# Layer 3's last two chunks of nodes summed over fetched lists of neighbours instead of a dense product

## The chip, the cores and the metric

The kernel runs on one core of one Trainium2 chip. The metric is device time in microseconds (us), lower is better. Times are the median of several executions; the profile is of one more execution.

## The reference, cut to what matters

A graph of 2708 nodes has 512 features per node (`x`) and a symmetric adjacency matrix `adj` of zeros and ones, with each edge drawn at a rate of about 0.006. Four layers run one after the other, each followed by a residual sum and a layer norm.

```python
x = _layernorm(x + L0(x, adj, deg))   # relu(((a_norm @ x) + x) @ W + b)
x = _layernorm(x + L1(x, adj))        # (dis * adj * dis) @ x @ W.T + b
x = _layernorm(x + L2(x, adj))        # two attention passes, below
x = _layernorm(x + L3(x, adj))

# L2, one pass: scores over all pairs, softmax, times adj, sum
a = softmax(Wh @ Ws.T) * adj; x = leaky_relu(a @ Wh + x)
# L3, eight heads whose weights lie side by side: in effect
L3 = (adj @ x) @ W + b
```

Layer 3 so needs, for every node, the sum of `x` over its neighbours, then one product with a 512x512 matrix.

## The kernel before, in words

The nodes are padded to 22 blocks of 128 (the last block has 20 nodes). They are taken in six chunks `CH` of 512, 512, 512, 512, 384 and 276 nodes: chunk 3 is blocks 12 to 15, chunk 4 blocks 16 to 18, chunk 5 blocks 19 to 21.

**Dense layers (0, 1 and 3).** `Fast.step` (line 1114) goes over steps (layer, chunk k, group g). A group is three or four blocks of neighbours. The adjacency lies in DRAM as bytes (`masks`, written in layer 0). `load` (762) fetches the bytes of a group two steps ahead on SP, `prepare` (807) casts them on ACT one step ahead to a page `m` (float32r, 128 neighbours x the chunk's nodes), and `multiply` (893) sums `x` over them on TensorE (PE): `x` is split into `hi` and `lo` so that the fast float32r product keeps its precision, and each block takes four matmuls for each of them, one for each 128 features. After six groups `evict` (967) copies the four sums to `ht`, already turned (features on the partitions). `project` (984) multiplies them with `W` one step later, and `combine`, `finish` (1056) and the DMA of the result follow. `residual` (1013) loads the rows for the residual sum (`xres`) on POOL's queue.

**Lists.** In layer 1 `index` (1183) builds for every block i the lists `givers[:, i, t]` of the neighbours that its nodes have. A block's twelve lists hold 128 row numbers each. Four of them (`t` from 8) serve the whole block, eight serve a quarter of 32 nodes (two lists each). `lists_of` (480) orders them: four single lists, then two groups with one list of each quarter. The last block has three single lists.

**Layer 2.** For each attention pass, `scores`, `soften` and `weigh` run as a pipeline over the chunks: PE computes the scores of chunk k, DVE and ACT make the softmax of chunk k-1 (times the byte mask `a`), and chunk k-2 is summed over its lists. `soften` (1606) writes the weights `s` with SP to a table `pairs` in DRAM, beside copies of the features; `fetch` (1660) gathers from it, with one indirect DMA per list on POOL, rows that hold both a neighbour's weights and its features. `weigh` (1715) multiplies the two parts of such a row on PE. A group of four quarter lists is four matmuls with 32 columns of weights side by side. At a chunk's end, `end` and `normalize` (1779) make the result rows `r` and write them to DRAM (`saved[2]`, the tile `x` of the DMA `x<-r`), from which layer 3 loads its rows again (`x<-x`).

**Order.** `Ordered` (54) keeps every engine's instructions in the order in which Python issues them, so each queue (PE, DVE, ACT, POOL and SP) works in order. All instructions are recorded at line 71. Where PE's order is a mixture of two strands, Python keeps a clock of estimated times (`advance`, `later`) and issues a piece when that clock says that its inputs are there. Layer 3's first three chunks are begun inside layer 2's end (`early`, 604), since their first 16 neighbour blocks are ready then. Their groups 4 and 5 and all of chunks 3 to 5 come after it.

**Buffers.** `page` gives one of 82 buffers of 2 KB per partition. A new tile takes a buffer whose earlier tile has no more users in the program, and its first writer waits for those users. `wide` gives one of 11 buffers for gathered rows, `bank` one of eight PSUM banks in two halves of four.

The lines at layer 2's end that write the result:

```python
for (i, _, _), (r, _) in zip(ch.blocks, ch.ends):
    self.nc.sync.dma_start(self.k.saved[2][i], r)
    self.made[i] = r
```

Of the kernel before, what the change touches and what calls it, by code (L numbers as in the profile page):

```python
# [8 lines left out]
FP = mybir.dt.float32  # L9
# [32 lines left out]
FAR = 4096  # L42
PAGES, WIDES = 82, 11
TWO = 3
LN_EPS = 1e-5
DEG_EPS = 1e-8
SLOPE = 0.01
# [40 lines left out]
class Kernel:  # L88


    def __init__(self, ctx, tc, x_in, x_t, adj, adj_t, w0, b0, w1, b1, w2, w2_t, w3, b3, out):
        self.tc, self.nc = tc, tc.nc
        nc = self.nc
        self.ctx = ctx
        self.x_in, self.x_t, self.adj, self.adj_t, self.out = x_in, x_t, adj, adj_t, out
        self.w0, self.b0, self.w1, self.b1, self.w2 = w0, b0, w1, b1, w2
        self.w2_t, self.w3, self.b3 = w2_t, w3, b3
        const = ctx.enter_context(tc.tile_pool(name="const", bufs=1))
        self.small = ctx.enter_context(tc.tile_pool(name="small", bufs=4))
        scratch = ctx.enter_context(tc.tile_pool(name="scratch", bufs=1, space=DRAM))  # L100
        tile_ = lambda name, shape, dt: const.tile(shape, dt, tag=name, name=name)
        self.ident = tile_("ident", [P, P], FP)
        self.ones = tile_("ones", [P, P], FP)
        self.ones_b = tile_("ones_b", [P, P], BF)

        self.rdeg = tile_("rdeg", [P, NB], FP)
        self.dis = tile_("dis", [P, NB], FP)
        self.nbad = len(CH) * NB
        self.bad = tile_("bad", [P, self.nbad + NB], FP)


        self.feeds = tile_("feeds", [P, NB, QUARTERS, NB], BF)
        self.givers = tile_("givers", [P, NB, LISTS], I32)

        self.base = tile_("base", [P, QUARTERS], FP)
        self.upto = tile_("upto", [P, P], BF)
        self.node = tile_("node", [P, 1], FP)
        self.block = tile_("block", [P, NB], BF)
        self.since = tile_("since", [P, P], BF)
        self.saved = [  # L120
            [scratch.tile([P, D], FP, tag=f"x{s}_{i}", name=f"x{s}_{i}") for i in range(NB)]
            for s in range(3)
        ]
        self.between = [
            scratch.tile([P, D], FP, tag=f"y_{i}", name=f"y_{i}") for i in range(NB)
        ]

        self.masks = [
            scratch.tile([P, NB, w], U8, tag=f"mask{k}", name=f"mask{k}")
            for k, (_, w) in enumerate(CH)  # L130
        ]

        self.turned = [
            [
                scratch.tile([P, DC, w], FP, tag=f"t{s}_{k}", name=f"t{s}_{k}")
                for k, (_, w) in enumerate(CH)
            ]
            for s in range(2)
        ]
# [345 lines left out]
    return rest + [[q * ONLY + t for q in range(QUARTERS)] for t in range(ONLY)]  # L485


def cost(columns):

    return 4 * columns / 2400  # L490
# [25 lines left out]
class Fast:  # L516
# [17 lines left out]
    def run(self):  # L534
        kernel, nc = self.k, self.nc
        with ExitStack() as ctx:
            pool = lambda name, bufs, **kw: ctx.enter_context(
                self.tc.tile_pool(name=name, bufs=bufs, reuse_waits="tile", **kw)
            )
            self.pages, self.wides = pool("pages", PAGES), pool("wides", WIDES)  # L540
            self.small, self.lists = pool("small_f", 4), pool("lists", 1)
            self.banks = [pool(f"banks{h}", 4, space=PSUM) for h in range(2)]
            given = [kernel.x_in[bass.ts(i, P), :] for i in range(NB)]
            l0 = Layer(0, given, kernel.w0, kernel.b0)
            l1 = Layer(1, kernel.saved[0], kernel.w1, kernel.b1)
            l3 = Layer(3, kernel.saved[2], kernel.w3, kernel.b3)
            self.attention = attention = Attention(self)
            self.jobs, self.due, self.other, self.beats = [], None, 1, 0
            run = Run(l0, l1)
            for t in range(len(run.seq)):  # L550
                self.step(run, t)
            attention.project(attention.layers[0], 0)
            for g in range(3):
                self.ends(run, g)
                if g == 1:
                    attention.project(attention.layers[0], 1)


            run = Run(l3)
            run.seq = [(l3, k, g) for k in range(TWO) for g in range(4)]  # L560
            run.seq += [(l3, k, g) for g in (4, 5) for k in range(2)]
            run.seq += [(l3, k, g) for k in range(2, TWO) for g in (4, 5)]
            run.seq += [(l3, k, g) for k in range(TWO, len(CH)) for g in range(len(GROUPS))]
            attention.run(self.early(run))
            for j in range(*GROUPS[5]):
                l3.rows[j] = attention.made[j]
            for t in range(4 * TWO, len(run.seq)):
                self.step(run, t)

            ly, k = run.before  # L570
            parts = self.project(ly, k)
            for some in (parts[:-1], parts[-1:]):
                made = []
                for i, n, ps in some:
                    made.append((i, n, self.combine(ly, k, len(made), i, n, ps)))
                self.finish(ly, k, made)
# [230 lines left out]
    def prepare(self, ly, k, g, between=None, late=False):  # L807
# [7 lines left out]
        for j, at in zip(range(*GROUPS[g]), ats):  # L815
            if k == 0:
                self.halve(ly, j)
            m = self.page(f"m{ly.number}_{k}_{j}", FR)
            nc.scalar.copy(m[:, :cw], at[:, :cw])
            ms.append(m)  # L820
            if between:
                between()
                between = None
# [7 lines left out]
        if ly.number == 1:  # L831
            at = ly.done.pop(("bytes", k, g))
            if late:
                return lambda: self.note(k, g, at)
            self.note(k, g, at)

    def note(self, k, g, at):

# [54 lines left out]
    def multiply(self, ly, k, g, only=None, ds=range(DC)):  # L893
# [9 lines left out]
        if blocks[-1] == NB - 1:  # L903


            blocks = blocks[:-1]
            for x in (ly.hi, ly.lo):
                for d in range(DC):
                    few = slice(d * QW, (d + 1) * QW)
                    nc.tensor.matmul(  # L910
# [102 lines left out]
    def residual(self, ly, k):  # L1013
        for i, _, _ in blocks_of(k):
            t = self.page(f"xres{ly.number}_{i}")
            self.nc.gpsimd.dma_start(t, ly.source[i])
            ly.done["xres", i] = t

    def biased(self, ly, k):
# [94 lines left out]
    def step(self, run, t):  # L1114
# [5 lines left out]
            self.attention.blank()  # L1120
        if ly.number == 1 and k == len(CH) - 1 and g in (2, 3, 4):
            self.attention.begin(g - 2)
        self.multiply(ly, k, g)
        if g == len(GROUPS) - 1 and k in ly.begun:
            self.evict(ly, k)
        wide = CH[k][1] == BANK
# [1 line left out]
            self.work("PE")  # L1128
        if run.before:
            self.ends(run, run.phase)  # L1130
            run.phase += 1
            if run.phase in ((3, 4, 5) if wide else (4,)):
                self.work("DVE")
# [234 lines left out]
class Attention:  # L1368
# [29 lines left out]
    def blank(self):  # L1398
# [3 lines left out]
        for pairs in (p for ly in self.pairs for p in ly):  # L1402
            self.nc.sync.dma_start(
                pairs[N:, : 2 * PAIR + D].rearrange("j (r d) -> j r d", d=D),
                t[:n, :].unsqueeze(1).to_broadcast([n, (2 * PAIR + D) // D, D]),
            )

    def begin(self, step):

# [369 lines left out]
    def normalize(self, ch):  # L1779
# [4 lines left out]
        def rest():  # L1784
            for _ in work:
                pass
            for (i, _, _), (r, _) in zip(ch.blocks, ch.ends):
                self.nc.sync.dma_start(self.k.saved[2][i], r)
                self.made[i] = r

        self.later(4, rest)
# [111 lines left out]
            yield from self.project_steps(ly, k)  # L1903


@with_exitstack
def kernel(
    ctx: ExitStack,
# [60 lines left out]
```

## Time and profile before

| | |
|---|---|
| median of 3 runs | 2306.28 us (2305.75 to 2307.77) |
| the profiled execution | 2307.16 us, span 2305.3 us |
| granted TensorE clock, mean | 0.995 |
| busy: PE, DVE, ACT, POOL | 2272.8, 1409.5, 675.9, 706.5 us |
| moved by DMA | 486.34 MB, mean 211 GB/s |
| gathers `g<-pairs,givers` on POOL | 510, mean 1031 ns; 6.1 us from issue to landing |

A line of the profile gives line, engine, operation, the tiles written and read (`out<-in`), shapes, a count, and the time. In a timeline the first two columns are start and length in us, and in brackets stands the engine's idle time before the piece with what ended it. In the chain of work that ended last the columns are start and length. "SPq" is the queue of SP, which issues DMAs; the length there is that of the issue, not of the transfer. A float32 matmul stands as two records.

Layer 1 ends near 605 us, layer 2's second pass runs from about 1250 to 2095, and after that only layer 3 is at work.

### The profile page before, as it was taken

The page shows a single profiled execution, that of the slowest core. Times are in us where ns is not written, and L with a number is a line of the kernel's source. Part 1 is how long each engine was busy: PE and PEld are TensorE (multiplying, and loading weights), DVE is VectorE, ACT ScalarE, POOL GpSimd, SP SyncE. Part 2 cuts the span into 40 slices and gives each one's busy share as a digit, 9 for nine tenths or more (in the row PEclk, how much of TensorE's full clock was granted, in tenths as well). Part 3 has the DMA queues.
Part 4 walks back from the last instruction along what each step waited for, and adds up shares of the span by engine and source line. Part 5 has one row for each costly group of instructions (what it writes and reads, how often), then busy time and mean ns, then how long its engine had stood idle before and what let it go on. Part 6 is the DMA issues. An engine that isn't in the chain of part 4 may idle for free.

```text
span 2305.3 us, 25891 instructions
## 1 busy us (share of the span) xinstructions
PE 2272.8 (99%) x8525; PEld 1292.4 (56%) x8525; DVE 1409.5 (61%) x2803; ACT 675.9 (29%) x1354; POOL 706.5 (31%) x822
## 2 busy tenths in 40 slices
PE   9999999999999999999999999999999999899997
PEld 6676777778644444443555444444443455476685
DVE  6777886786554538748667511228769789625523
ACT  7444352323111123222332200113222334342211
POOL 3333431111000001635466550001635467542000
PEclk9999999999999999999999999999999999999999
DMA  9966762222556505868699998504868799973311
GB/s 347 288 189 179 188 182 76 76 82 77 194 191 263 182 5 181 296 205 300 236 331 336 337 411 320 185 5 165 301 228 288 250 324 332 338 219 120 117 51 43
DMA packets 260929, 486.34 MB, mean 211 GB/s; under 512 B 40238, under 2 KB 126950, under 8 KB 260784
## 3 DMA queue, kind: packets, MB, share of 16 engines
q1 hardware_dynamic: 192128, 269.63, 33.6%
q0 software_dynamic: 68656, 214.96, 28.0%
q8 instruction: 69, 1.13, 0.2%
q14 instruction: 76, 0.62, 0.1%
HBM read 307.55 MB, written 176.92 MB: 210 GB/s over the span
## 4 chain that ended last, share of the span: by engine, by line
PE 87%; DMA 5%; DVE 4%; issue 2%; ACT 1%; POOL 1%; SPq 0%; DVEq 0%; POOLq 0%; ACTq 0%
PE sp L71 33%; PE acc L71 30%; PE mm L71 8%; PE z L71 6%; PE wst L71 6%; DMA at<-in_adj_t 1%; DMA g<-pairs,givers 1%; PE mix L71 1%; DMA xr<-y 1%; PE list L71 1%; DMA mask<-some 1%; DMA x<-x 0%; PE tr_x2t L71 0%; PE tr_x2b L71 0%; DVE xl L71 0%
## 5 line engine op out<-in xcount | busy, mean ns | idle before, releaser
L71 PE MATMUL sp<-xs,wst_sb 128*128 128x512 f32 (+3 forms) x2112 | 798.3, 545 | 0.0
L71 POOL DMA_INDIRECT g<-pairs,givers x510 | 525.6, 1031 | 870.6 <-DMA xr<-x 242.3
L71 PEld LDWEIGHTS sp<-xs,wst_sb 128*128 128x128 f32 (+1 forms) x2112 | 380.5, 186 | 407.7 <-issue 325.6
L71 PE MATMUL acc<-m,xh 128*128 128x512 f32 (+4 forms) x1584 | 567.8, 380 | 7.4 <-ACT m L71 5.8
L71 PE MATMUL acc<-m,xl 128*128 128x512 f32 (+4 forms) x1584 | 551.0, 366 | 3.5 <-DVE xl L71 3.5
L71 PEld LDWEIGHTS acc<-m,xh 128*128 128x128 f32 (+1 forms) x1584 | 288.6, 188 | 72.0 <-issue 21.6
L71 PEld LDWEIGHTS acc<-m,xl 128*128 128x128 f32 (+1 forms) x1584 | 289.1, 189 | 48.0 <-issue 5.5
L71 PE MATMUL acc<-g 128*32 128x512 f32 (+1 forms) x1020 | 265.7, 609 | 2.9 <-DMA g<-pairs,givers 2.5
L71 ACT COPY s<-sp 128x512 f32<-128x512 f32 (+2 forms) x252 | 132.6, 528 | 396.3 <-PE sp L71 389.8
L71 ACT ACTIVATE s<-s 128x512 f32<-128x512 f32 (+3 forms) x264 | 151.7, 580 | 323.5 <-DVE s L71 323.2
L71 DVE TENSOR_TENSOR top<-top,s 128x512 f32<-128x512 f32 (+2 forms) x240 | 149.4, 623 | 155.6 <-ACT s L71 153.9
L71 PE MATMUL mm<-w,ht 128*128 128x512 f32 (+1 forms) x528 | 224.1, 594 | 3.4 <-DVE ht L71 3.4
L71 ACT CAST m<-at 128x512 fp32r<-128x512 uint8 (+5 forms) x396 | 199.6, 567 | 60.9 <-DMA at<-mask 20.2
L71 DVE TENSOR_TENSOR s<-s,shift 128x512 f32<-128x512 f32 (+3 forms) x264 | 162.9, 620 | 38.2 <-ACT shift L71 38.2
L71 DVE TENSOR_TENSOR s<-s,a 128x512 f32<-128x512 f32 (+3 forms) x264 | 165.9, 628 | 15.1 <-DMA a<-mask 6.0
L71 DVE TENSOR_TENSOR sum<-sum,s 128x512 f32<-128x512 f32 (+4 forms) x252 | 156.9, 623 | 13.9 <-ACT s L71 13.9
L71 PEld LDWEIGHTS mm<-w,ht 128*128 128x128 f32 (+1 forms) x528 | 95.9, 186 | 121.2 <-issue 111.4
L71 PEld LDWEIGHTS acc<-g 128*32 128x32 f32 (+1 forms) x1020 | 75.8, 135 | 146.1 <-issue 118.0
L71 PE MATMUL z<-w,xt 128*128 128x512 f32 (+1 forms) x352 | 151.0, 596 | 0.0
L71 PE MATMUL wst<-xt,mixed 128*128 128x512 f32 (+2 forms) x384 | 150.5, 545 | 0.0
L71 POOL DMA_DIRECT2D x<-o x44 | 26.0, 597 | 354.8 <-DVE o L71 350.6
L71 PEld LDWEIGHTS wst<-xt,mixed 128*128 128x128 f32 x384 | 72.1, 190 | 71.0 <-issue 59.0
(168 smaller groups left out, 1495.3 us busy)
## 6 DMA issues: line engine op xcount, KB each, us to landing
pairs<-z_sb SPq DMA_DIRECT2D x84, 768.0 KB
pairs<-s SPq DMA_DIRECT2D x168, 256.0 KB
at<-in_adj_t SPq DMA_DIRECT2D x84, 256.0 KB
xres<-x POOLq DMA_DIRECT2D x44, 256.0 KB, 4.9
x<-o POOLq DMA_DIRECT2D x43, 256.0 KB, 2.9
pairs<-s SPq DMA_DIRECT2D x84, 128.0 KB
x<-x SPq DMA_DIRECT2D x37, 256.0 KB
at<-mask SPq DMA_DIRECT2D x32, 256.0 KB
```

The lines of the kernel that those rows point to most:

```text
L71: ins = call(*args, **kw)
```

## The change

Chunks 0 to 3 of layer 3 stay dense. For chunks 4 and 5 (six blocks, from `LISTED` = 16) the neighbours' rows are fetched by list, as in layer 2, with zeros and ones in the place of the attention weights.

A new table `sided` in DRAM has a row for every node: three times 128 values for an even block, 512 features, 128 values for the odd block after it. The values are the adjacency as float32.

- `blank` (layer 0) writes zeros to the pad rows, with four DMAs.
- `prepare` calls `give` for every cast page `m` of layer 1's chunks 4 and 5: two DMAs per page on SP, 88 in all.
- `normalize` in layer 2's second pass writes each block's `r` three times over into `sided`, with one DMA of 768 KB per block on SP, right behind the write to `saved[2]`.
- `Listed`, made when the attention has ended, fetches the 63 lists of the six blocks (10 ahead), beginning with block 21. While chunk 3's groups 1 to 5 run, `multiply` is called for one feature block d at a time, and `beside` puts lists in between, up to 1.6 times the dense piece's time. A block's sum leaves PSUM by DVE, is turned by four PE transposes, copied by ACT, and projected. `end_all` issues what is left, and chunk 3's projection comes after it.
- The residual rows of layer 3 are loaded on SP instead of POOL.

```diff
+DENSE = 4
+LISTED = CH[DENSE][0] // P
+SIDED = D + 2 * P
...
-            run.seq += [(l3, k, g) for k in range(TWO, len(CH)) for g in range(len(GROUPS))]
+            run.seq += [(l3, k, g) for k in range(TWO, DENSE) for g in range(len(GROUPS))]
             attention.run(self.early(run))
             for j in range(*GROUPS[5]):
                 l3.rows[j] = attention.made[j]
+            self.listed = Listed(self, l3)
             for t in range(4 * TWO, len(run.seq)):
                 self.step(run, t)
+            self.listed.end_all()
 
             ly, k = run.before
             parts = self.project(ly, k)
...
+            if ly.number == 1 and k >= DENSE:
+                self.give(k, j, m)
...
+    def give(self, k, j, m):
+
+        n, lo, cw = rows_of(j), 0, CH[k][1]
+        while lo < cw:
+
+            i = (CH[k][0] + lo) // P - LISTED
+            w = min(P if i % 2 == 0 else 2 * P, cw - lo)
+            at = i // 2 * SIDED + i % 2 * (D + P)
+            self.nc.sync.dma_start(
+                self.k.sided[j * P : j * P + n, at : at + w], m.bitcast(FP)[:n, lo : lo + w]
+            )
+            lo += w
...
-            self.nc.gpsimd.dma_start(t, ly.source[i])
+            (self.nc.sync if ly.number == 3 else self.nc.gpsimd).dma_start(t, ly.source[i])
...
-        self.multiply(ly, k, g)
+        if self.listed and k == DENSE - 1 and g > 0:
+            for d in range(DC):
+                self.multiply(ly, k, g, ds=[d])
+                self.listed.beside(few_us(k, g) / DC)
+        else:
+            self.multiply(ly, k, g)
+            if self.listed:
+                self.listed.advance(few_us(k, g))
...
                 self.nc.sync.dma_start(self.k.saved[2][i], r)
+                rows = self.k.sided[i * P : (i + 1) * P, P:]
+                self.nc.sync.dma_start(
+                    bass.AP(
+                        rows.tensor,
+                        rows.offset,
+                        [rows.ap[0], (SIDED, (NB - LISTED) // 2), (1, D)],
+                    ),
+                    r.unsqueeze(1).to_broadcast([P, (NB - LISTED) // 2, D]),
+                )
                 self.made[i] = r
...
+    def beside(self, us):
+
+        self.advance(us)
+        end = self.clock + 1.6 * us
+        while self.clock < end and self.weigh():
+            pass
...
+            nc.gpsimd.indirect_dma_start(
+                out=g[:, :width],
+                out_offset=None,
+                in_=self.k.sided[:, :],
+                in_offset=bass.IndirectOffsetOnAxis(ap=self.k.givers[:, i, t : t + 1], axis=0),
+                element_offset=(i - LISTED) // 2 * SIDED + first,
+            )
+            self.free = max(self.free, self.clock) + 1.3
+            self.fetched.append((g, self.free + 6))
...
+        for h, g in enumerate(gs):
+            lo, rows = (h * QW, QW) if side else (0, n)
+            e, z = (D + lo, 0) if odd else (0, P - lo)
+            nc.tensor.matmul(
+                self.acc[lo : lo + rows],
+                g[:, e : e + rows],
+                g[:, z : z + D],
+                start=first,
+                stop=last,
+            )
+        self.advance(1.1 if side else cost(D))
+        if last:
+            acc = self.acc
+            self.later(0, lambda: self.turn(i, n, acc))
+        self.fetch_ahead()
+        return True
...
+    def turn(self, i, n, acc):
+
+        nc, f = self.nc, self.f
+        r = f.page(f"sum3_{i}")
+        nc.vector.tensor_copy(r[:n], acc[:n])
+
+        def turn():
+            ps = f.bank(self.half, f"tr3_{i}", (P, DC, P))
+            for c in range(DC):
+                nc.tensor.transpose(
+                    ps[:, c, :n], r[:n, bass.ts(c, P)], self.k.ident[:n, :n]
+                )
+            t = f.page(f"turned3_{i}", FP, (P, DC, P))
+            nc.scalar.copy(t[:, :, :n], ps[:, :, :n])
+            x = self.ly.done["xres", i]
+            nc.vector.tensor_add(x[:n], x[:n], self.ly.bt[:n])
+            self.advance(0.45)
+            self.later(2, lambda: self.project(i, n, t))
+
+        self.later(2, turn)
```

## The prediction

> **What bounds the kernel now.** I read the page first. Its first line of busy times says that TensorE (PE) works nearly the whole span, so a change pays if it takes PE work away and costs only where it makes PE wait.
>
> ```profile
> PE 2272.8 (99%) x8525; PEld 1292.4 (56%) x8525; DVE 1409.5 (61%) x2803; ACT 675.9 (29%) x1354; POOL 706.5 (31%) x822
> ```
>
> Next came the chain of work that ended last, in order of time. Its last pieces are layer 3's end, with PE back to back:
>
> ```profile
> 2163.00 13.73 PE mm L71 x32
> 2176.73 37.30 PE acc L71 x176
> 2214.03 13.73 PE mm L71 x32
> 2227.76 28.38 PE acc L71 x176
> 2256.14 10.30 PE mm L71 x24
> 2266.44 18.06 PE acc L71 x143
> ```
>
> A float32 matmul stands as two records; four of them make the `mm` of a 128-row block (13.73 us for four blocks). The first `acc` piece is chunk 3's groups 1 to 5 (144 matmuls) and chunk 4's group 0 (32). The next is the rest of chunk 4 with chunk 5's group 0, the last is the rest of chunk 5. Chunk 5's `mm` follows and ends at 2292.97; DVE work and the write of the result fill the time to 2305.3.
>
> Where does PE wait before that? The windows of 5 us between 1780 and 2110 show holes almost only from 1950 to 2020, where layer 2 ends and layer 3 begins. Columns: PE, PEld, DVE, ACT, POOL busy, granted clock, DMA share, GB/s.
>
> ```profile
> 1975.00:1980.00 5.00, 3.25 (x7) 0.46 (x6) 0.00 (x0) 0.63 (x1) 3.78 (x5) 0.84 1.03 409
> 1995.00:2000.00 5.00, 5.00 (x23) 4.13 (x22) 4.83 (x14) 1.86 (x5) 0.00 (x0) 1.00 1.01 354
> 2000.00:2005.00 5.00, 1.58 (x7) 1.01 (x6) 4.59 (x11) 2.72 (x7) 0.00 (x0) 1.00 0.63 186
> ```
>
> The DMA engines are full (share about 1) from 1910 to 2000. The timelines of SP, ACT, DVE and PE in that stretch give the mechanism:
>
> ```profile
> 1987.17 2.63 SPq L71 DMA_DIRECT2D x<-r  x4
> 1991.66 3.02 SPq L71 DMA_DIRECT2D x<-x  x4
> ...
> 1992.32 0.62 ACT L71 CAST m<-at 128x512 fp32r<-128x512 uint8 x1 [6.96 <-DMA x<-r]
> ...
> 1993.32 0.55 DVE L71 COPY sum<-s 128x276 f32<-128x276 f32 x1 [0.54 <-DMA x<-r]
> ...
> 2003.54 0.61 ACT L71 ACTIVATE xh<-x 128x512 fp32r<-128x512 f32 x1
> ...
> 2004.71 0.50 PE L71 MATMUL acc<-m,xh 128*128 128x512 f32 x1 [3.42 <-ACT m L71]
> ```
>
> Chunk 3 of layer 2 writes its four result blocks `r` (12 to 15) at 1987. The new tiles `xl`, `m` and `sum` take over the pages of those `r` and wait until the writes have read them. After `sum`, DVE and ACT alternate over chunk 5's softmax, and only behind that does ACT prepare layer 3's next group, for which PE waits 3.42 us. So **the release of those pages sets when PE goes on**: 2004.71 is 11.4 us after `sum` could start.
>
> **What the Trainium skill says.** "DMA: Bandwidth & Descriptors", section Queues, rings and completion order: each of the 16 DMA engines goes round the queues that have work, and takes descriptors of one queue in ring order; a large write therefore holds back what SP issues behind it. The trace agrees: one 256 KB `xr<-y` that SP issued at 1973.53 landed 13.20 us later by the chain. "Perfetto Trace Analysis", section DMA Instruction — HWDGE (DVE, Sync): the profiled slice of such a DMA is the making of descriptors, not the movement of data. Here a `x<-r` slice is about 0.34 us and the page is free some 6 us later. "TensorE: Matmul & The Clock Gate", Part 1: an idle TensorE falls to half its clock until it has been busy again; here the clock was 0.66 in 2005 to 2010, after the 3.42 us.
>
> **Part 1: layer 3's end.** Removed: the dense sums of chunks 4 and 5. Chunk 4 is 5.5 (group 0) + 24.3 (28.38 less chunk 5's group 0 of 4.1), chunk 5 is 4.1 + 18.06: **51.9 us of PE**. Their 44 casts on ACT and mask loads on SP lay beside it: nothing.
>
> Added: blocks 16 to 20 have four single lists and two groups of four quarter lists each, block 21 three single lists. A single list is one float32 128x512 matmul, 0.858 us (13.73 / 16); a group of four took 0.99 to 1.12 in layer 2 (the `acc` x8 pieces of the chain between 1830 and 1949). So 23 x 0.858 + 10 x 1.1 = 30.7. Six turns of four transposes at 0.45 (`tr_top` x4 took 0.44): 2.7. The projections move but stay 18.0 in sum. **51.9 - 30.7 - 2.7 = 18.5 us less PE.**
>
> Do the lists arrive? 63 gathers on POOL, ten of them fetched ahead. The step of POOL is 0.95 + 0.30 = 1.26 us where no buffer is missing:
>
> ```profile
> 2036.14 0.95 POOL L71 DMA_INDIRECT g<-pairs,givers  x1 [0.30 <-PE acc L71]
> 2037.40 0.95 POOL L71 DMA_INDIRECT g<-pairs,givers  x1 [0.30 <-issue]
> ```
>
> The other 53 start when chunk 3's group 1 does and need 66.8 us, landing 6.1 us after issue (median of the page), so 73 us. PE has beside them 32 us of dense work, 30.7 of lists, 2.7 of turns and 18 of projections, 84 in all, and the order was built for 1.3 us per gather. I take 0.3 us of waiting. Exposed is the last block alone: PE waits for DVE's copy (0.95) and ACT's copy (0.8), with chunk 3's projection queued behind. The old wait of about 0.2 for `ht` goes. Three blocks instead of two are normalised ahead of the last one: 0.4. DVE and ACT queues delay some turns: 0.9, from nothing to 3. Sum: -18.5 + 0.3 + 1.75 - 0.2 + 0.4 + 0.9 = **-15.3, between -17 and -11**, the lower gain if a gather takes 1.4 us, as in 1840 to 1850.
>
> **Part 2: layer 2's copies.** Behind every `x<-r` SP issues a copy of 768 KB, 22 in all, 16.9 MB. At the 0.40 MB/us that the windows show for full DMA that is 42 us of DMA time, in bursts of 3.1 MB (7.7 us) at 1700, 1799, 1896, 1987, 2056 and 2102. SP's issue (0.36 us, as for `pairs<-z_sb`) is hidden, since SP mostly waits.
> - 1700 and 2056: idle DMA follows (0.13 in 1720 to 1725, 0.36 in 2060 to 2065) before anything is due: 0.
> - 1799: the masks `a` queue behind. They are due at 1819.66 and come near 1823; DVE is full until 1880, then has nearly 4 us to spare (1.19 busy in 1880 to 1885). 0.5, from 0 to 3.
> - 1896: about 2.4 MB fit into the gaps to 1925; 0.7 MB stays queued until 1987.
> - 1987: `r` of block 14 is free after 3.07 MB in SP's ring instead of 0.77, beside some 2.5 MB of gathers and the 0.7 left. 1987.3 + 14 (5.6 MB at 0.4) + 1.7 + 2 for the receipt (0.77 MB at half the rate is 3.9 of the 6 us seen) gives 2005, against 1993.3. PE goes on 11.4 us after that, at 2016. **+11.3, between +4 and +18**: +4 if SP's ring is served at full rate.
> - 2102: ACT's casts wait for those pages too; the page frees 2 to 6 us later, where the casts at 2108.75 are about 4 us ahead of PE's use at 2113.7: 0.5, up to 4.
>
> Sum **+12.3**.
>
> **Part 3: layer 1's writes.** 88 small DMAs on SP, each waiting for a cast on ACT. SP spends 88 x 0.45 = 40 us in some 85, so it keeps up, but what is queued behind is late. Near the end the casts of group 3 run at 589.43, their eight writes end near 593.5, then come eight weight loads (3.8 us), the last mask load at 597, six writes, and `xt` at 600.5.
>
> ```profile
> 589.43 1.38 ACT L71 CAST m<-at 128x276 fp32r<-128x276 uint8 x4
> ...
> 595.21 2.05 ACT L71 CAST m<-at 128x276 fp32r<-128x276 uint8 x6
> ```
>
> The mask lands near 601 (its cast is due at 594.66 + 4.1 + 3.0, the start of group 3 and the length of groups 3 and 4: 601.8) and `xt` near 605.5 to 606.5 (PE wants it at 604.90, "PE wst"). **+2, from 0 to 6.** Four blanking writes in layer 0, whose SP is busy with `at` loads: +0.3, up to 1.5. `xres` moves from POOL to SP: its waits for pages now hold up mask loads behind it, but chunk 3 runs at half its pace there, so they come in time: 0, up to 2.
>
> **Sum against the profiled execution** (2307.16 us, span 2305.3): -15.3 + 12.3 + 2.0 + 0.3 = -0.7, so 2306.5. That execution lies 0.9 above the median of the three runs (2306.28), so the sum on the median is 2305.6. I say 2306.
>
> **Rivals.**
> - *A wash (0.40)*: the sum above, with a range of its own of 2301.7 to 2310.9. Within 0.2% (4.6 us) is about what a measurement of this kernel can tell from no change.
> - *Faster: the copies are absorbed (0.27).* If SP's ring gets most of the DMA engines at 1987, `sum` starts 4 us later and the rest is as above: -15.3 + 5 + 2.3 = -8, **2298**. For it: three `x<-r` landed within 6 us of the first issue though DMA was full. Against: windows show 1.03 with 409 GB/s, nothing left to take.
> - *Slower: the copies crawl (0.33).* SP's ring moved only about 0.17 MB/us while gathers ran (0.41 less a gather of about 0.3 MB per 1.26 us). If gathers keep that share throughout, 3.8 MB take 22 us, `sum` starts at 2011, PE at 2022.5: +18 instead of +11.3, in all +6, **2312**. It decides once block 14's page frees more than 16 us late. For it: the 13.20 us for one small load. Against: POOL's gathers stop at 1993.7, so the engines are free for SP from about 2000.
>
> The smaller unknowns (layer 1, the turns, a slower gather) push up more than down. **Range 2296 to 2317**, from a little past the faster rival to a little past the slower one. Chances: faster 0.27, same 0.40, slower 0.33.
>
> **What would show it.** Right: chunk 3's lists and dense work fill PE without a hole over 1 us; the last `mm` ends about 16 us earlier relative to PE's start on chunk 3's group 0; a hole of 12 to 15 us in PE near 2001 to 2016, with `sum` waiting for the new copy. Wrong in the first part: waits for `g` in layer 3. Wrong in the second: `sum` starts within 5 us of 1993. Wrong in the third: PE waits before 610, over 5 us.

## The result and the profile after

The changed kernel takes **2323.73 us** (median of 4, 2322.02 to 2325.5). The kernel before takes 2307.03 (median of 4, among them the three that stand in the table of before). The ratio is 1.0073, with a 95% interval of 1.006 to 1.0086: slower by some 17 us. The profiled execution took 2322.38 us with a span of 2320.3, so it is 15.0 us longer in the span than the one of before. Helper lines have moved: what was L71 is L76, and L75 in kernels that only add a table to the kernel before.

The page's first line of busy times answers to the one shown of before:

```profile
PE 2263.3 (98%) x8323; PEld 1255.0 (54%) x8323; DVE 1412.1 (61%) x2812; ACT 661.4 (29%) x1313; POOL 756.0 (33%) x863
```

PE is busy for 9.5 us less, though the span is 15 us longer, so about 24.5 us of new idle time has come in. Busy time is not work alone: matmuls that a lowered clock stretches count in full, and the mean granted clock is 0.990 instead of 0.995. To find where the time went, I compare the start of the same PE instruction in both traces (chain of waits and timelines). The lag is by how much it starts later in the changed kernel:

| stage that ends there | before | after | lag | step of lag | predicted |
|---|---|---|---|---|---|
| layer 0's last products | 359.55 | 361.02 | 1.5 | +1.5 | +0.3 |
| layer 1 (first `wst`) | 604.90 | 616.58 | 11.7 | +10.2 | +2.0 |
| layer 2's end | 2016.20 | 2035.33 | 19.1 | +7.4 | +12.3 |
| chunk 3 of layer 3 begins | 2176.73 | 2195.87 | 19.1 | 0 | 0 |
| end of the span | 2305.3 | 2320.3 | 15.0 | -4.1 | -15.3 |

The last row belongs to the chain's end. In the changed kernel it reads, in order of time from the last list sums (start, length, what):

```profile
2260.70 9.12 PE acc L76 x43
2269.82 0.44 PE tr L76 x4
2270.26 2.65 PE acc L76 x8
2272.91 3.45 PE mm L76 x8
2276.38 0.70 DVE xres L76
2277.10 0.71 DVE st L76
2278.01 2.38 DVE xres L76 x4
2280.39 1.20 DVE ht L76 x2
2281.59 0.61 DVE sum L76
2282.24 1.13 PE tr L76 x4
2283.40 0.59 ACT turned L76
2284.03 16.33 PE mm L76 x32
```

The dense `acc` of chunks 4 and 5 is gone, and in this stretch PE is back to back until 2276. Then the chain leaves PE for DVE: the four additions of chunk 3's bias and two copies of `ht` stand in DVE's queue ahead of the copy `sum` for which PE waits.

At layer 2's end, the windows after (columns as in the prediction):

```profile
2010.00:2015.00 5.00, 3.75 (x17) 2.77 (x16) 3.07 (x8) 1.25 (x3) 0.00 (x0) 1.00 1.03 399
2015.00:2020.00 5.00, 3.59 (x16) 2.63 (x14) 4.86 (x14) 1.78 (x5) 0.00 (x0) 1.00 1.06 392
2020.00:2025.00 5.00, 1.15 (x3) 0.61 (x3) 4.37 (x10) 3.48 (x8) 0.00 (x0) 0.75 0.81 269
```

PE's hole lies near 2020 and is about as deep as the one of before at 2000 to 2005 (1.58 busy). It lies some 20 us later, as does the end of full DMA, and the lag there is 19.1 us. So the hole has hardly grown, and the one of 12 to 15 us that the prediction named isn't there.

### The profile page after: what moved, and what is told of

It is laid out like the page before. It is cut to its first block, busy times and chain, and to the rows that moved or that the text cites. A ratio compares the mean times of both kernels' runs of the same rounds, so it can differ in the third digit from the quotient of the medians.

```text
span 2320.3 us, 25746 instructions
## 1 busy us (share of the span) xinstructions
PE 2263.3 (98%) x8323; PEld 1255.0 (54%) x8323; DVE 1412.1 (61%) x2812; ACT 661.4 (29%) x1313; POOL 756.0 (33%) x863
## 4 chain that ended last, share of the span: by engine, by line
PE 82%; DMA 6%; DVE 5%; issue 3%; POOL 2%; ACT 1%; SPq 0%; POOLq 0%; DVEq 0%; ACTq 0%
PE sp L76 31%; PE acc L76 27%; PE mm L76 8%; PE z L76 6%; PE wst L76 6%; DMA g<-pairs,givers 2%; DMA pairs<-s 1%; DMA mask<-some 1%; DMA sided<-r 1%; DVE s L76 1%; POOL xt L76 1%; PE mix L76 1%; DMA x<-x 1%; PE list L76 1%; ACT m L76 0%
## 5 line engine op out<-in xcount | busy, mean ns | idle before, releaser
L76 POOL DMA_INDIRECT g<-pairs,givers x510 | 524.8, 1029 | 870.2 <-DMA pairs<-s 312.3
L76 PE MATMUL sp<-xs,wst_sb 128*128 128x512 f32 (+3 forms) x2112 | 798.3, 544 | 0.0
L76 PEld LDWEIGHTS sp<-xs,wst_sb 128*128 128x128 f32 (+1 forms) x2112 | 379.7, 186 | 408.4 <-issue 326.6
L76 PE MATMUL acc<-m,xh 128*128 128x512 f32 (+3 forms) x1408 | 523.6, 392 | 15.4 <-ACT m L76 14.3
L76 PE MATMUL acc<-m,xl 128*128 128x512 f32 (+3 forms) x1408 | 503.1, 374 | 4.2 <-DVE xl L76 4.2
L76 PE MATMUL acc<-g 128*32 128x512 f32 (+2 forms) x1146 | 299.0, 608 | 6.1 <-DMA g<-pairs,givers 5.8
L76 PEld LDWEIGHTS acc<-m,xh 128*128 128x128 f32 (+1 forms) x1408 | 258.4, 190 | 84.7 <-issue 25.9
L76 PEld LDWEIGHTS acc<-m,xl 128*128 128x128 f32 (+1 forms) x1408 | 258.8, 190 | 50.9 <-issue 7.4
L76 ACT ACTIVATE s<-s 128x512 f32<-128x512 f32 (+3 forms) x264 | 151.7, 580 | 326.4 <-DVE s L76 326.1
L76 ACT COPY s<-sp 128x512 f32<-128x512 f32 (+2 forms) x252 | 132.7, 528 | 392.7 <-PE sp L76 387.6
L76 DVE TENSOR_TENSOR top<-top,s 128x512 f32<-128x512 f32 (+2 forms) x240 | 149.1, 621 | 155.3 <-ACT s L76 153.4
L76 PE MATMUL mm<-w,ht 128*128 128x512 f32 (+1 forms) x480 | 205.2, 593 | 4.0 <-DVE ht L76 4.0
L76 ACT CAST m<-at 128x512 fp32r<-128x512 uint8 (+5 forms) x352 | 183.4, 579 | 80.8 <-DMA at<-mask 29.0
L76 DVE TENSOR_TENSOR s<-s,shift 128x512 f32<-128x512 f32 (+3 forms) x264 | 162.7, 620 | 32.8 <-ACT shift L76 32.8
L76 DVE TENSOR_TENSOR s<-s,a 128x512 f32<-128x512 f32 (+3 forms) x264 | 165.9, 629 | 17.2 <-DMA a<-mask 8.2
L76 PEld LDWEIGHTS acc<-g 128*32 128x32 f32 (+2 forms) x1146 | 84.7, 135 | 165.7 <-issue 135.4
L76 DVE TENSOR_TENSOR sum<-sum,s 128x512 f32<-128x512 f32 (+4 forms) x252 | 156.6, 621 | 15.6 <-ACT s L76 15.6
L76 PE MATMUL z<-w,xt 128*128 128x512 f32 (+1 forms) x352 | 151.0, 596 | 0.0
L76 PE MATMUL wst<-xt,mixed 128*128 128x512 f32 (+2 forms) x384 | 150.5, 544 | 0.0
L76 PEld LDWEIGHTS mm<-w,ht 128*128 128x128 f32 (+1 forms) x480 | 88.1, 187 | 112.6 <-issue 102.9
L76 POOL DMA_DIRECT2D x<-o x44 | 26.0, 598 | 369.2 <-DVE o L76 365.0
L76 PEld LDWEIGHTS wst<-xt,mixed 128*128 128x128 f32 x384 | 72.0, 190 | 71.1 <-issue 58.8
```

The source lines that it names most:

```text
L76: ins = call(*args, **kw)
```

## Experiments

The runs of a set stand on one chip beside the kernel before, and each ratio is to those. On some chips the kernel before itself took 2323 to 2329 us, with longer stretches at the attention passes' ends, so times are compared as ratios, and single traces by the step of the lag inside one stage. The changed kernel stands beside the kernel before in one set alone. Where a repair is set against its 1.0073, the two ratios can come from different chips, and the step in the trace stands beside it.

### Layer 1: the writes on SP

Theory: the 88 writes stand on SP ahead of the last mask. The changed kernel's SP queue:

```profile
583.33 0.41 SPq L76 DMA_DIRECT2D at<-mask  x1
591.38 3.75 SPq L76 DMA_DIRECT2D sided<-m  x8
595.22 0.81 SPq L76 DMA_DIRECT2D w<-in_w  x1
...
600.53 1.23 SPq L76 DMA_DIRECT2D mixed<-mixed  x1
601.85 0.55 SPq L76 DMA_DIRECT2D at<-mask  x1
```

and its chain of waits there:

```profile
601.85 8.12 DMA at<-mask
...
610.07 1.08 ACT m L76 x3
611.14 0.04 issue
611.19 4.81 PE acc L76 x23
```

SP sits idle from 583.7 to 591.4, waiting for the casts that the writes read. Behind them come the eight writes and eight weight loads, and the mask is issued only at 601.85. In the kernel before:

```profile
582.76 0.32 SPq L71 DMA_DIRECT2D at<-mask  x1
```

After the change the mask lands in full DMA after 8.12 us (its three casts start at 610.07), and PE waits 8.0. Its clock falls to 0.60 and 0.50 in the windows from 605 to 615, and the lag rises by 10.2, so the wait is partly paid twice.

**e1_gives**: the kernel before plus the table, its blanking and the writes; nothing reads them.

```diff
+            if ly.number == 1 and k >= DENSE:
+                self.give(k, j, m)
```

> The kernel before, with the new table, its blanking and the 88 writes of layer 1's casts, and nothing that reads the table. Theory A (the order on SP): the last mask of layer 1 and the features for layer 2 are issued behind the writes, which wait for casts: PE starts on layer 2's first product (wst) at about 616.5 instead of 604.9, and the whole is about 11.5 us slower than before (2318 to 2319), about 1.5 of it ahead of layer 1's last chunk. Rival B (the loss at layer 1's end in the changed kernel has another source than these writes, such as the longer program): within 3 us of before.

Measured 1.0065 (1.0035 to 1.0094) on a chip where before takes 2323: +15 us (8 to 22). In the trace the lag rises by 9.8 us between 595 and 606, with PE waiting 8.29 for the last casts. The writes alone make the loss of this stage; the rest of the median's 15 us isn't explained, but the interval takes in 9.8.

**e3_late_gives**: the changed kernel, each group's writes issued one step later, behind that step's loads, and layer 2's first loads (`begin`, the weights) ahead of them.

```diff
-                self.give(k, j, m)
+                self.given.append((k, j, m))
...
+            self.attention.begin(g - 2)
+        for job in self.given:
+            self.give(*job)
+        self.given = []
         if t + 1 < len(seq) and seq[t + 1][0].number == ly.number:
             self.prepare(*seq[t + 1])
```

> The changed kernel, with each group's 88 writes held back by one step, so that SP issues the mask and the loads for layer 2 ahead of them; number and size of all transfers are the same. Theory A (order on SP): layer 1's end gives back 8 to 10 us: wst starts near 607, the whole is 2314 to 2316. Rival B (the DMA engines are simply full there, so the order matters little): at most 3 us gained, 2320 or more.

Measured 1.0033 (1.002 to 1.0046): 9.3 us under the changed kernel's 1.0073. The queue of SP in this kernel:

```profile
582.03 0.38 SPq L76 DMA_DIRECT2D mixed<-mixed  x1
582.51 5.64 SPq L76 DMA_DIRECT2D sided<-m  x8
588.56 0.86 SPq L76 DMA_DIRECT2D at<-mask  x1
```

The weights are through by 582.4 and the last mask leaves at 588.56, 13 us earlier than in the changed kernel, and the lag stays at 1 us between 595 and 606. The bytes are the same, so it is **the order on SP**, not the load on the DMA engines.

### Layer 2: the copies

**e2_copies**: the kernel before plus the table and all 22 copies.

```diff
                 self.nc.sync.dma_start(self.k.saved[2][i], r)
+                self.nc.sync.dma_start(bass.AP(rows.tensor, ...), r.unsqueeze(1).to_broadcast(...))
```

> The kernel before, with the new table and the 22 copies of 768 KB at layer 2's end alone. Theory A: pages wait for the copies of blocks 12 to 15 once, and the whole is about 7.5 us slower than before (2314 to 2315), the hole in PE near 2000 to 2013. My predicted term was +12.3: 2319. Rival B (the lost time there comes from the lists' gathers or from the residual rows on SP): within 2 us of before.

Measured 1.0026 (1.0015 to 1.0038): +6.0 us (3.5 to 8.8). The copies alone cost; my +12.3 lies outside.

**e6_dram**: the changed kernel, each chunk's copies issued with the next chunk's end and read from the rows in DRAM. **e5_before** is the kernel before itself, for a trace on the same chip.

```diff
-                self.nc.sync.dma_start(bass.AP(rows.tensor, ...), r.unsqueeze(1)...)
+                self.owed.append((i, r))
...
+            for i, r in owed:
+                self.side(i, self.k.saved[2][i])
```

> The changed kernel, with each chunk's copies at layer 2's end issued one chunk later and read from the rows already in DRAM (the last chunk's from the pages), so that no page waits for them; at 1987 as many bytes go behind the writes as in the changed kernel (chunk 2's in the place of chunk 3's). Theory A (the page release sets when PE goes on): no wait for a copy in the new layer's first tiles, PE goes on 6 to 8 us earlier, 2316 to 2318. Rival B (the DMA engines' load or SP's queue sets it): at most 2 us gained, 2322 or more, with the rows of layer 3 (x<-x) arriving late behind the copies.

> The kernel before, unchanged, for a profile on the same chip as the next ones: every theory expects the time of before; POOL's last drain about 4.3 us, PE's step of layer 2's end as in the first profile or, if this chip moves data more slowly, a few us later.

Measured for e6_dram 1.0062 (1.0041 to 1.0082), 2.6 us under the changed kernel's ratio with overlapping intervals: taking the page wait away gave little, which speaks against my step. (e5_before took 2320.27, its drain 4.3 us; its lag to the first profile rises by 7 us at the end of layer 2 with nothing changed, so single traces of that chip settle nothing there.) The next three divide the copies on the kernel before, by `if ch.k in (...)` ahead of the copy.

**e9_ends** (chunks 0, 1, 4, 5):

> The kernel before, with the table and the copies of chunks 0, 1, 4 and 5 alone (14 of 22, 10.8 MB). Theory A (only the copies at 1896 and 1987 fall into full DMA engines and cost): within 1.5 us of before. Rival B (every copied byte costs about alike): 14/22 of the 6 us that all copies cost, so 3.8 us slower.

Measured 1.0000 (0.9992 to 1.0009). These 14 copies cost nothing that shows; 1.0 us was predicted.

**e10_third** (chunk 2):

> The kernel before, with the table and the copies of chunk 2 alone (four, at about 1896). Theory A1 (the pages of blocks 12 to 15, at 1987, set the loss): within 1 us of before. Rival B (the bytes queued on SP from 1896 on, which delay the weights and gathers of the last chunks): 3 us slower or more. My prediction priced these copies at nothing by themselves.

Measured 1.0023 (1.0015 to 1.003): **+5.3 us**. I had given these copies nothing. Behind them SP writes chunk 4's softmax weights, 44 writes up to 1957. The first ten of them after the copies, in the kernel before:

```profile
1900.17 9.79 SPq L71 DMA_DIRECT2D pairs<-s  x10
```

and in e10_third:

```profile
1900.73 1.24 SPq L75 DMA_DIRECT2D sided<-r  x1
1902.33 12.63 SPq L75 DMA_DIRECT2D pairs<-s  x10
```

From 1900 to 1915 DMA is full (share 1.02 to 1.06, in the kernel before 0.61 to 0.93), and SP itself slows down: one issue of a copy takes 1.24 us. The weights' writes end later, and POOL comes to wait for them ahead of the first gather that reads them, in e10_third and in the kernel before:

```profile
1961.71 1.46 POOL L75 DMA_INDIRECT g<-pairs,givers  x1 [5.41 <-DMA a<-mask]
```

```profile
1959.69 0.95 POOL L71 DMA_INDIRECT g<-pairs,givers  x1 [0.30 <-DMA a<-mask]
```

This gather waits for several queues in a row; the profile names `a<-mask`, the load that SP issues right behind the writes. Then PE waits for a gathered row (timeline of PE in e10_third):

```profile
1969.50 8.56 PE L75 MATMUL acc<-g 128*128 128x512 f32 x14 [4.02 <-DMA g<-pairs,givers]
```

All waits for gathered rows from 1880 to 2025 come to 6.0 us there, and to 1.9 in the kernel before. Whether the writes are late by SP's slower issue or by the full engines isn't separated.

**e11_fourth** (chunk 3):

> The kernel before, with the table and the copies of chunk 3 alone (four, at about 1987). Theory A1: the whole loss of 6 us. Rival B: 2 to 3 us slower, the rest belonging to chunk 2's copies. My prediction priced these at +11.3.

Measured 1.0004 (0.9996 to 1.0012): +0.9 us (-0.9 to 2.8). With 0.0 and 5.3 the three parts come to 6.2, against 6.0 for all 22 copies. The page wait on which I had put +11.3 exists, but is short (timeline of DVE in e11_fourth):

```profile
1992.08 0.69 DVE L75 SCALAR_TENSOR_TENSOR xl<-x,xh 128x512 fp32r<-128x512 f32 x1 [3.47 <-DMA sided<-r]
1992.69 0.44 DVE L75 TENSOR_TENSOR s<-s,shift 128x276 f32<-128x276 f32 x1
1993.05 0.29 DVE L75 COPY sum<-s 128x276 f32<-128x276 f32 x1
```

`xl` waits for the first copy alone, and `sum` finds its page free, at 1993.05. The changed kernel shows the same (lines of ACT and DVE):

```profile
2008.45 0.62 ACT L76 CAST m<-at 128x512 fp32r<-128x512 uint8 x1 [7.66 <-PE acc L76]
2011.86 0.69 DVE L76 SCALAR_TENSOR_TENSOR xl<-x,xh 128x512 fp32r<-128x512 f32 x1 [5.96 <-DMA sided<-r]
2012.83 0.29 DVE L76 COPY sum<-s 128x276 f32<-128x276 f32 x1
```

In the kernel before, `m` and `sum` waited for `x<-r` too. Now `m` waits for PE and `sum` for nothing: going by their waits, they have taken other pages than those of the `r` being copied.

**e13_third_later**: the changed kernel with chunk 2's copies moved to chunk 4's end (2056), read from DRAM.

```diff
+                if ch.k != 2:
+                    self.side(i, r)
...
+            for i, _, _ in blocks_of(2) if ch.k == 4 else ():
+                self.side(i, self.k.saved[2][i])
```

> The changed kernel, with chunk 2's four copies alone moved from about 1896 to the end of chunk 4, about 2056, read there from the rows in DRAM; all others stay, chunk 3's at 1987 on its pages too. Theory A (in the changed kernel too the loss at layer 2's end comes from chunk 2's copies): ratio to before 1.0045 to 1.005, so 5 to 6 us better than the changed kernel. Rival B (together with the rest it is the pages at 1987 that decide): at most 1 us better, 1.007 or more.

Measured 1.0045 (1.0033 to 1.0058), 6.5 us under the changed kernel's ratio; the lag rises by 3.1 us from 1945 to 2020 instead of 7.7. So in the changed kernel too chunk 2's copies are most of that stage's loss. It would also explain e6_dram, where chunk 1's copies had taken chunk 2's place.

### Layer 3: its end

**e4_end**: the changed kernel; chunk 3's bias a group earlier (and its residual rows loaded two groups earlier), its four projections around the last list block's turn.

```diff
+            while listed.to_weigh:
+                listed.weigh(True)
+            for n, b in enumerate(blocks_of(k)):
+                parts += self.project(ly, k, [b])
+                listed.advance((3, 3, 3, 0)[n])
...
+        if last and g == 4:
+            self.biased(ly, k)
```

> The changed kernel, with the order at layer 3's end altered: chunk 3's bias is added a group earlier, its four projections stand around the last list block's transposes and projection, and two of its sums come earlier on VectorE. Theory A (PE waits 4 us for VectorE's copy of the last block's sum and then runs at a lowered clock): the wait of 4.0 and the slow mm of block 20 (6.0 instead of 3.4) vanish: 6 us gained, 2317 to 2318. Rival B (the program's end, not PE, sets the last 12 us): at most 2 us gained. Rival C: the loss of clock comes back elsewhere: about 4 us gained.

Measured 1.0048 (1.003 to 1.0065): 5.8 us under the changed kernel's ratio, with intervals that touch. The timeline of PE in the changed kernel (in brackets the wait):

```profile
2282.24 1.12 PE L76 MATMUL tr<-ident,sum 128*128 128x128 f32 x4 [4.05 <-DVE sum L76]
2284.03 6.02 PE L76 MATMUL mm<-w,turned 128*128 128x512 f32 x8 [0.68 <-ACT turned L76]
```

and in e4_end, where these pieces have no wait:

```profile
2298.58 0.60 PE L76 MATMUL tr<-ident,sum 128*128 128x128 f32 x4
2299.01 3.60 PE L76 MATMUL mm<-w,ht 128*128 128x512 f32 x8
2302.45 3.60 PE L76 MATMUL mm<-w,turned 128*128 128x512 f32 x8
```

The same eight records take 3.60 instead of 6.02 us: after 4.05 us of waiting the granted clock was 0.63 from 2285 to 2290. From chunk 3's beginning to PE's end it takes 103.2 us instead of 107.75, so the trace shows 4.5 us of the gain.

### The program's end: POOL's drain

From the last `o` (it ends at 2297.5 before, at 2308.5 after) to the end of the span lie 7.8 us before and 11.8 after. Two queues are at work there: SP waits until the last results have landed and then has a short drain instruction, and POOL has a long one. Both stand at the program's last line (min/median/max in ns, start of the first and of the last), in the kernel before and in the one after:

```profile
L1965 POOLq DRAIN  x3: 46/103/4315, 2300.1 to 2305.0; - x3
L1965 SPq DRAIN  x3: 7/7/13, 2303.8 to 2304.7; - x3
```

```profile
L2173 POOLq DRAIN  x3: 46/103/7663, 2311.8 to 2320.0; - x3
L2173 SPq DRAIN  x3: 7/7/13, 2314.3 to 2319.7; - x3
```

Before, SP is through at 2303.8 and POOL's long drain ends at 2304.4, so the write of the result nearly hides it. After, SP is through at 2314.3 and POOL at 2319.4.

Kernels that add gathers to the kernel before, whose rows nothing uses:

```diff
+                if t == len(run.seq) - 8:
+                    for e in range(32):
+                        self.nc.gpsimd.indirect_dma_start(out=self.wide(f"extra{e}")[:, :D], ...)
```

**e7_late_gather** (one), **e12_32_gathers** (32), **e15_16_gathers** (16) and **e16_63_gathers** (63, spread over 13 of the last 17 steps):

> The kernel before, with one gather more on POOL in layer 3's last chunk, whose result is not used. Theory A (POOL's drain at the program's end takes longer where gathers were issued shortly before): the time from the last o to the end rises from 7.8 to about 11.8 us, the drain from 4.3 to about 7.6. Rival B (it takes longer for the number of gathers, 573 instead of 510, or for the other code): it stays within 0.5 us of 7.8.

> The kernel before, with 32 gathers more on POOL beside chunk 4 of layer 3, whose rows are not used. Theory A (the drain at the end grows with each gather issued after layer 2; 3.3 us for 63, 0.05 each): drain about 6.0 us, from the last o to the end about 9.8. Rival B (it comes with the lists' code or with a number over some bound): drain 4.3 to 4.4, or the full 7.6.

> The kernel before, with 16 gathers more beside chunk 4 of layer 3, whose rows are not used. The drain at the end was 4.3 us with none, 4.4 with one, 6.9 with 32. Theory A (it grows with the gathers issued late, about evenly): drain about 5.6 us. Rival B (a step somewhere between 1 and 32): 4.4 or 6.9.

> The kernel before, with 63 gathers more, spread over layer 3's chunks 3 to 5 like the lists of the changed kernel, whose rows are not used. Theory A (the number of late gathers alone makes the changed kernel's drain of 7.7 us): drain 7.4 to 7.9 and 11.5 to 12 us from the last o to the end. Rival B (the changed kernel's code or its residual rows on SP have a part): 1 us or more away from that.

Measured drains: 4.40, 6.93, 5.62 and, for 63, **0.80** us (their times, 2323.64, 2309.56, 2311.23 and 2305.09, are single runs on three chips and aren't compared). In e16_63_gathers:

```profile
L1974 POOLq DRAIN  x3: 46/103/803, 2297.8 to 2303.0; - x3
L1974 SPq DRAIN  x3: 7/7/13, 2302.4 to 2302.7; - x3
```

Here SP comes last, and from the last `o` to the end lie 7.2 us: of the 7.8 before, the drain of 4.3 made only about 0.6.

So neither recency nor the number of gathers is the rule. My theory fell at 63: the changed kernel has as many more gathers and a drain of 7.66. What fits is the number of all POOL DMAs, 774 before and 815 after (63 gathers more, 22 residual loads fewer): 4.32 + 0.082 for each one more gives 4.40, 5.63, 6.94 and 7.68 for 1, 16, 32 and 41 more, as measured (4.40, 5.62, 6.93, 7.66). Between 41 and 63 it starts over.

**e17_pool_rows**: the version e14_three (below) with the 22 residual loads on POOL again (`self.nc.gpsimd` for `self.nc.sync` in `residual` and `fetch_ahead`), so 63 more.

> The version with all three repairs, with the residual rows of layer 3 (22 DMAs) on POOL's queue again. So far the last drain fits 4.3 us plus 0.082 for each DMA more on POOL than in the kernel before (1, 16, 32 and, in the changed kernel, 41 more), and it starts over between 41 and 63 more: 63 gave 0.8. This kernel has 63 more. Theory A (the count of POOL's DMAs alone sets the drain): drain about 0.8 us, 7.2 from the last o to the end instead of 11.7, ratio 0.9945 to 0.996, if POOL's 22 issues delay no gather that PE waits for. Rival B (the drain has to do with gathers and their rows alone): drain 7.7 or 9.5, ratio 0.997 or more.

The drain was 0.80 us, as the count says: the 22 loads, which are no gathers, took it there from 7.66, so they count too. But the ratio was 1.001 (0.9995 to 1.0025). Behind the lists' first gathers on POOL the residual rows came late; waits of PE (us in total, times, longest):

```profile
PE acc L76 <- DVE xres L76: 6.8, 2, 5.8
```

So the move to SP, which I had priced at 0, spares a loss that I had not seen.

**e18_count**: e14_three with 24 other DMAs on POOL instead (65 more).

```diff
+            queue = self.nc.gpsimd if ly.number == 0 and k else self.nc.sync
+            queue.dma_start(t[:, : CH[k][1]], self.k.turned[ly.number][k][:, c, :])
...
-            self.nc.sync.dma_start(sided[N:, lo:hi], t[:n, : hi - lo])
+            self.nc.gpsimd.dma_start(sided[N:, lo:hi], t[:n, : hi - lo])
```

> The version with all three repairs, with 24 other DMAs moved from SP to POOL: the features of chunks 1 to 5 for layer 2's first pass (20) and the blanking of the new table (4). POOL is nearly idle at both places, and the residual rows of layer 3 stay on SP. POOL has 65 DMAs more than in the kernel before. Theory A (the count sets the drain, starting over between 42 and 63): drain 0.8 to 1.3 us, about 4.3 us off the time of the version it starts from, ratio 0.995 (0.994 to 0.996). Rival B (the loads come late on POOL, where they queue behind the writes of layer 1's last results): PE waits near 680 and the ratio is 0.997 or more.

The drain was 0.97 us (0.80 and two more), from the last `o` to the end 7.0 us, and no load came late. The ratio was 0.9986 (0.9971 to 1.0002), not the 0.995 expected. It stands on another chip than e14_three, and its trace lost time in the attention passes, as e5_before's did with nothing changed. The drain's worth is thus shown in the trace and not in the ratio.

This kernel shows the four blanking writes too. SP in the kernel after:

```profile
76.96 10.29 SPq L76 DMA_DIRECT2D sided<-blank  x4
87.38 22.17 SPq L76 DMA_DIRECT2D at<-in_adj_t  x26
```

and in e18_count:

```profile
77.87 31.55 SPq L76 DMA_DIRECT2D at<-in_adj_t  x26
```

Four small writes hold SP for 10 us, and the adjacency loads stand behind them. From 88 to 105 us the lag to the first profile changes by -1.5 to 3.2 us in the nine kernels that have them on SP (median 1.4), by -1.5 or -1.1 in the nine without, and by -1.2 in e18_count. So they can cost up to 4.7 us, but in the changed kernel's own profile (-1.1) they cost at most 0.4.

### All repairs together

**e8_all**: e3, e4, and chunks 2's and 3's copies moved to chunk 4's end. **e14_three**: the same, but with only chunk 2's moved.

> The changed kernel with all three repairs: layer 1's writes held back a step, layer 3's end reordered, and the copies of chunks 2 and 3 issued with chunk 4's, from DRAM, where the DMA engines have gaps. If the three losses are independent (9 + 6 + 7.5 of 16.8), it is 4 to 6 us faster than before: 2301 to 2303. Rival B (the copies' bytes cost time wherever they are placed, or the losses hide one another): 2307 to 2312, no faster than before.

> The changed kernel with chunk 2's copies moved as in the run beside it, layer 1's writes held back a step and layer 3's end reordered. Theory A (three independent losses, of which 9.3, 5.8 and 5.3 us come back of 16.8): 3 to 4 us faster than before, ratio 0.998 to 0.9985. Rival B (the losses hide one another): ratio 1.000 or more.

Measured for e8_all 0.9984 (0.9969 to 1.0000): between no change and -7 us. Measured for e14_three **0.9969 (0.996 to 0.9979), 2299.32 against 2306.6**: 7.1 us faster than the kernel before, more than the 3 to 4 expected, and some 24 faster than the change. The three repairs measured one by one give 9.3 + 5.8 + 6.5 = 21.6; the sum agrees within their intervals, so there is no sign that one loss hides another. POOL's drain is still 7.66 here. The only wait of PE left in its layer 3 end is 1.7 us for a `sum` behind DVE's normalisation.

## Why the prediction was wrong

The forecast was 2306 between 2296 and 2317; the result lies 7 us above the range, on the side of the slower rival but not by its mechanism. Two terms failed by their size: the cost of layer 1's writes (+2.0, measured +10.2) and the waits and the end of layer 3 (-15.3, measured -4.1). Layer 2's term (+12.3, measured +7.4) came near by luck: the wait on which it stood costs little, and copies priced at nothing cost most. By the prediction's steps:

- **PE's work in layer 3: right.** Less waits and slow clock, the stretch from chunk 3's group 0 to the last `mm` took about 98 us (107.75 - 6.4 - 3.1); the prediction's 116.2 - 18.5 is 97.7. In e14_three, with most waits gone, it took 100.0, so 16.3 less than before. The gathers held their 1.26 us step where a buffer was free, and PE never waited for them.
- **Layer 3's delays: mis-sized, 1.75 + 0.9 + 0.3 in the sum.** PE waited 1.69 + 4.05 + 0.68 = 6.4 us (expected 2.95), since I counted the copies' own lengths and not what stood ahead of them in DVE's order: a normalisation at 2217 and six pieces of chunk 3's end at 2278. I had named chunk 3's bias nowhere. The clock after the wait cost some 3.1 more (the last five blocks of `mm` took 19.59 us instead of 5 x 3.43, `tr` 1.13 instead of 0.44), though I had cited the Trainium skill's page on the clock gate ("TensorE: Matmul & The Clock Gate", Part 1) for another place. Together 6.6 of the 11.2 missing.
- **"DVE work and the write of the result fill the time to 2305.3": nearly right for the kernel before, but I took the stretch behind the last `o` for constant, and 41 more DMAs on POOL for free.** They lengthened POOL's drain by 3.3 us, and a semaphore instruction ahead of it by 0.8, past the write of the result: 4.0 of the 11.2.
- **Layer 1, +2.0: mis-sized, +10.2.** I had the order on SP right (the mask behind casts, writes and weight loads) and put the mask's issue at 597 and its landing at 601. It was issued at 601.85: 1.5 us of this is lag that was there already, and the eight weight loads took 6.5 us instead of 3.8 (up to 1.56 each). Then it took 8.12 us to land instead of 4. Part 3 had the mask due at 601.8, so nothing was left to absorb this.
- **Layer 2 at 1987, +11.3: wrong.** In the changed kernel only `xl` waits for a copy, that of block 12, the first in the ring. `sum`, for which I had counted on block 14's page behind 3.07 MB, waits for no copy. Alone these copies cost 0.9 (e11_fourth). In the changed kernel `xl` waited 5.96 us at 2011.86, `sum` followed at once, and PE's lag rose by 2.0 from 1975 to 2020. The range given (+4 to +18) began above that.
- **Layer 2 at 1896, "0.7 MB stays queued": priced at nothing, and the largest term of that stage**, +5.3. I asked what SP's ring still held at 1987, and not what stood behind the copies in it: the weights that chunk 4's gathers wait for. The rival "the copies crawl" looked at the wrong burst.
- **1700, 1799, 2056, 2102: right**, 0.0 (e9_ends, -1.8 to 2.1).
- **Blanks, +0.3: neither right nor wrong by this pair.** The lag of +1.5 in the profiled pair does not come from them: it arises at 335 us, where the other kernels, with and without blanks, step by -1.5 to +0.3, and its cause stays open. **`xres` on SP, 0: right**, and the other way would have cost.

So the predicted sum -0.7 became +15.0: +1.2 (layer 0, cause open), +8.2 (layer 1), -4.9 (layer 2) and +11.2 (layer 3) against the terms. Layer 1's miss is a price taken from quiet stretches: issues at 0.45 us and a landing after 4, where the windows from 595 to 605 show DMA shares of 0.87 and 1.02.

## What to carry to other kernels

A DMA that waits for a cast blocked everything that SP had to issue later (7.6 us idle ahead of layer 1's last writes): put urgent loads ahead of it, or delay it by a step, which costs no bytes. In a stretch where the DMA engines are full, price added traffic by what is queued behind it and who waits for that, up to the next real gap; the same bytes were free at 2056. When PE's last stretch depends on a copy by DVE, count everything ahead of it in DVE's order and leave PE other work to do meanwhile, since the wait is partly paid again in clock (4.05 us of waiting, 3.1 more behind it).

## What the hardware showed that was not expected

- POOL's drain at the program's end took from 0.80 to 7.66 us, by 0.082 us for each DMA that POOL had issued (774 gave 4.32, 815 gave 7.66), and started over by 837 (0.80). Loads and gathers count alike. Up to 4.3 us it was nearly hidden behind the landing of the last results. What it counts inside a DMA, and where exactly it starts over, wasn't tried.
- SP's issue of a DMA took 0.3 to 0.4 us in most places and up to 1.2 to 1.6 us in bursts at a DMA share of 0.87 to 1.06 (the copies at 1900 in e10_third, a weight load at 598.92 in the changed kernel). Full engines alone don't slow it: in the kernel before, single loads at 1973.53 and 1975.32 were issued in 0.32 us at a share of 1.03. Four small blanking writes held SP for 10.3 us at a share of only 0.8. What sets the time of an issue wasn't tried.
